# Two preact attention layers in float32: one-pass sums, a different order of VectorE's additions, and the last batch's order

## The chip, the cores and the metric

The kernel runs on one core of one Trainium2 chip. The metric is the device time of the whole kernel in microseconds, from one launch, as the median of several runs. Lower is better. The core's engines are called as in the profile: PE (TensorE, matrix products), DVE (VectorE), ACT (ScalarE), POOL (GpSimd) and SP (SyncE, which here only issues DMAs).

## The reference

The input x has 8 batches of 32 x 32 positions (1024 tokens) and 512 channels, all float32. Two residual layers follow one another. Each normalises its input over groups of 16 channels, runs an attention and adds the result to its input.

```python
# layer 0: 16 heads of 32
x = x + attention_0(group_norm(x))      # softmax(q k^T * 32**-0.5) v, then @ w_proj + b_proj
# layer 1: 4 heads of 128, relative position logits
x = x + attention_1(group_norm(x))      # q = x @ Wq * 128**-0.5
                                        # scores = q k^T + rel_w(q, pos_w) + rel_h(q, pos_h)
                                        # softmax(scores) v, then @ Wo
```

## The kernel before, in words

**Layout.** Activations are kept transposed, channels on the 128 partitions and 1024 tokens along the row, as blocks of 4 x 1024 (eight such blocks in SBUF). Every projection of a 512 x 512 matrix is done by a seven-product scheme (`seven`, called through `project_T`, `project_rows` and the output projections): the operand is split into quarters a11, a12, a21, a22; `forms` makes four sums of them on DVE (lines 339 to 342, 128x1024 each); seven products, each of half the channels, go to PSUM banks x, y, z in the order 0, 5, 1, 4, 6, 2, 3. One such run makes half the output and is called a unit. Bank y is a running sum: after product 5 DVE reads it (`a`, line 379), then product 4 is added on top and DVE reads it again (`b`, line 387), then product 2. So PE may not start product 4 before `a` has been read. Products 0 and 1 use a11 and a12 alone and need none of the forms.

**First attention** (`attention_0`): 64 steps per batch (4 head groups, 2 halves of the queries, 8 key tiles). A step makes the scores of four heads into the four-bank PSUM tile `ps` (line 539), ACT exponentiates them to `e` (line 547, 128x2048, two buffers, tag `e0`), PE multiplies the `e` of the step before with the values (line 558), and DVE adds that `e` to the running `esum` (lines 567 and 569). After 8 steps the sums over keys are a product with ones (line 579), and `normalise` turns them into factors (lines 502 to 524: an ACT copy, two DVE transposes, a reciprocal, a POOL multiplication).

**Second attention** (`attention_1`): 64 steps per batch (4 heads, 2 halves, 8 key tiles). A step is a float32 product of keys and queries (line 654), a float32r product that adds the position logits (line 655), an exponential (line 657, buffers of tag `e1`, three of them), the values product (line 666) and DVE's addition (lines 675 and 677). Every 8 steps a float32 product with ones (line 686) gives the sums, in one of the three PSUM banks of tag `bank`, followed by `normalise`.

**Order.** The main loop runs nine rounds. In round b, `side_by_side` spreads the rest of the work evenly over the steps of batch b's first attention: the output projection of batch b-1's first layer (`after_0`), that of batch b-2's second layer (`after_1`, with its output transposes at line 856 and the DMAs at line 861), the second norm (`norm_1`, scalings at line 294), the projections of `second`, batch b-1's second attention and the projections of batch b+1. The steps of the second attention have no cost in this spreading, so in most rounds all 64 stand between two steps of the first attention. `load` of the next batch is woven into them, one piece every six steps. Round 7 has no next batch and interleaves the first 32 steps of the second attention with the first attention. Round 8 has only the rest. After it stands the last `after_1`, of batch 7. Weights are loaded by SP some products ahead (lines 193 and 197), in program order with SP's other DMAs: outputs, inputs, and the copies of x put away in DRAM (line 218) and fetched back (line 225).

**Queues.** [...] The framework orders instructions from the program and from dependences; `tc.issue_after(x)` keeps what it encloses behind x.

**Start.** `load_first` loads batch 0 in rows, transposes it on PE (line 744), copies it from PSUM (lines 752 and 754), takes statistics (line 249), puts x away, normalises in place (line 294) and makes the forms. `add_up` (line 146) makes the four differences of each weight matrix that the seven products need.

## Time and profile before

| | us |
|---|---|
| median of 3 runs | 3877.97 (3873.93 to 3879.32) |
| the profiled execution | 3877.0 |
| its span, first to last instruction | 3875.2 |
| PE busy | 3803.0 (98%) |
| DVE busy | 2516.4 (65%) |
| ACT busy | 1723.9 (44%) |
| POOL busy | 625.1 (16%) |
| TensorE clock granted, mean | 0.996 |

A row of the page or of an answer names the line of the kernel, the engine, the operation, what it writes and from what, with tile names. `x512` counts instructions; busy time and mean duration follow, then the idle time of the engine just ahead and what ended it. In the timeline the first number is the start, the second the time taken, and a bracket at the end gives idle time before and its releaser. A float32 product appears as two records. Records of PE overlap in time, [...] so a busy PE can still hide short waits.

### The profile page before, as it was taken

What the parts mean: (1) busy time and instruction counts of PE and PEld (TensorE: products, weight loads), DVE (VectorE), ACT (ScalarE), POOL (GpSimd) and SP (SyncE); (2) the same over time, 40 slices, a digit from 0 to 9 for tenths busy, and PEclk for the clock granted to TensorE, in tenths of its full rate; (3) what the DMA queues carried; (4) which work ended last, traced back from release to release, by engine and by line L of the source; (5) the groups of instructions that cost most, each with busy time, mean ns of one, the idle gap of its engine ahead of it and who ended that gap; (6) DMA issues with size and microseconds to landing.
All of it is one profiled execution on the core that took longest, in us unless ns stands there. A gap on an engine that the chain in (4) does not pass through costs nothing.

```text
span 3875.2 us, 79813 instructions
## 1 busy us (share of the span) xinstructions
PE 3803.0 (98%) x34478; PEld 1375.0 (35%) x34478; DVE 2516.4 (65%) x2905; ACT 1723.9 (44%) x1767; POOL 625.1 (16%) x400
## 2 busy tenths in 40 slices
PE   8999999999999999999999999999999999999998
PEld 3222244232443234432343323433234332334353
DVE  6777765686745867468664686656866568665544
ACT  2554543545434454344544445444453445553232
POOL 2242101121001211012111121111210112001101
PEclk9999999999999999999999999999999999999999
DMA  6122120142202322033120241103311023110401
GB/s 183 58 87 80 42 60 3 37 126 65 57 6 79 94 54 55 12 92 87 42 55 17 92 94 38 47 21 98 90 41 39 27 97 76 34 52 24 121 17 23
DMA packets 482984, 234.73 MB, mean 61 GB/s; under 512 B 269600, under 2 KB 461376, under 8 KB 481600
## 3 DMA queue, kind: packets, MB, share of 16 engines
q1 hardware_dynamic: 470992, 213.74, 20.4%
q0 software_dynamic: 2608, 13.70, 1.0%
q8 instruction: 274, 4.49, 0.5%
q10 hardware_dynamic: 9024, 2.10, 0.3%
q14 instruction: 86, 0.70, 0.1%
HBM read 170.72 MB, written 58.72 MB: 59 GB/s over the span
## 4 chain that ended last, share of the span: by engine, by line
PE 87%; DVE 8%; ACT 2%; issue 2%; DMA 0%; SPq 0%; POOL 0%; DVEq 0%; ACTq 0%; POOLq 0%
PE ps L539 12%; PE ps L654 11%; PE acc L666 11%; PE acc L558 11%; PE y_q L315 4%; PE y_v L315 4%; PE y_k L315 4%; PE ps L655 3%; PE x_q L315 3%; PE z_k L315 3%; PE x_v L315 3%; PE x_k L315 3%; PE z_q L315 3%; PE z_v L315 3%; DVE es L569 2%; ACT e L547 2%
## 5 line engine op out<-in xcount | busy, mean ns | idle before, releaser
L547 ACT ACTIVATE e<-ps 128x2048 f32<-128x2048 f32 x512 | 961.6, 1878 | 839.3 <-PE ps L539 628.2
L569 DVE TENSOR_TENSOR es<-es,e 128x2048 f32<-128x2048 f32 x384 | 893.3, 2326 | 408.6 <-ACT e L547 405.6
L539 PE MATMUL ps<-q,k 32*64 32x512 f32 x8192 | 576.6, 614 | 18.4 <-ACT e L547 18.4
L657 ACT ACTIVATE e<-ps 128x512 f32<-128x512 f32 x512 | 305.7, 597 | 573.8 <-PE ps L655 537.8
L558 PE MATMUL acc<-e,v 128*32 128x512 f32 x4096 | 545.9, 605 | 0.0
L654 PE MATMUL ps<-q,k 128*128 128x512 f32 x1024 | 525.2, 595 | 0.3 <-DVE posT L640 0.3
L666 PE MATMUL acc<-e,v 128*128 128x512 f32 x1024 | 522.0, 593 | 0.0
L524 POOL TENSOR_TENSOR q<-q,su 128x512 f32<-128x512 f32 x128 | 216.3, 1690 | 1556.8 <-DVE su L520 1538.0
L677 DVE TENSOR_TENSOR es<-es,e 128x512 f32<-128x512 f32 x384 | 290.6, 757 | 252.8 <-ACT e L657 250.8
L655 PE MATMUL ps<-posT,sel 128*128 128x512 f32 x512 | 407.0, 795 | 0.0
L654 PEld LDWEIGHTS ps<-q,k 128*128 128x128 f32 x1024 | 192.9, 190 | 250.4 <-issue 243.8
L539 PEld LDWEIGHTS ps<-q,k 32*64 32x64 f32 x8192 | 120.3, 130 | 409.8 <-issue 221.1
L666 PEld LDWEIGHTS acc<-e,v 128*128 128x128 f32 x1024 | 193.5, 190 | 146.3 <-issue 105.0
L558 PEld LDWEIGHTS acc<-e,v 128*32 128x32 f32 x4096 | 81.5, 108 | 412.0 <-issue 364.7
L567 DVE TENSOR_TENSOR es<-e,e 128x2048 f32<-128x2048 f32 x64 | 172.9, 2701 | 33.2 <-ACT e L547 33.2
L504 DVE STREAM_TRANSPOSE tu<-su 128x512 f32<-128x512 f32 x128 | 90.6, 708 | 121.7 <-ACT su L502 120.1
L502 ACT COPY su<-sums 128x512 f32<-128x512 f32 x128 | 74.9, 585 | 149.0 <-PE sums L579 81.2
L655 PEld LDWEIGHTS ps<-posT,sel 128*128 128x128 f32 x512 | 97.5, 190 | 122.3 <-issue 122.3
L640 DVE TENSOR_TENSOR posT<-pp,posT 32x512 fp32r<-32x512 f32 x128 | 112.0, 875 | 32.3 <-ACT posT L635 31.0
L675 DVE TENSOR_TENSOR es<-e,e 128x512 f32<-128x512 f32 x64 | 44.2, 691 | 135.8 <-ACT e L657 135.8
L428 POOL TENSOR_TENSOR k<-b_k,p_k 128x512 f32<-128x512 f32 x32 | 51.9, 1623 | 483.6 <-ACT p_k L393 483.6
L635 ACT CAST posT<-pp 32x512 fp32r<-32x512 f32 x128 | 106.2, 829 | 46.3 <-PE pp L622 45.1
(200 smaller groups left out, 4449.4 us busy)
## 6 DMA issues: line engine op xcount, KB each, us to landing
w_qkv<-ws_qkv SPq DMA_DIRECT2D x168, 128.0 KB, 2.5
d<-x0T SPq DMA_DIRECT2D x32, 512.0 KB, 3.6
x1T<-d SPq DMA_DIRECT2D x32, 512.0 KB, 5.4
d<-x1T SPq DMA_DIRECT2D x32, 512.0 KB, 3.4
x2T<-d SPq DMA_DIRECT2D x32, 512.0 KB, 6.0
w_qkv<-in_L_conv_w_qkv SPq DMA_DIRECT2D x126, 128.0 KB, 2.2
out<-ot SPq DMA_DIRECT2D x240, 64.0 KB, 2.0
xs<-in_x SPq DMA_DIRECT2D x224, 64.0 KB, 2.5
```

The costliest lines, as they stand in the source:

```text
L315: ins = nc.tensor.matmul(out[columns, :], weights[:, columns], moving, start=start, stop=stop, skip_group_check=open_sum,)
L524: nc.gpsimd.tensor_tensor(dst, dst, su, op=ALU.mult)
L539: nc.tensor.matmul(ps[some, r, :], k[m][rows, j * P + 64 * i : j * P + 64 * i + 64], q[m][rows, h * NB : (h + 1) * NB], start=True, stop=True,
L547: nc.scalar.activation(e, ps, AF.Exp, scale=D0 ** -0.5)
L558: nc.tensor.matmul(acc[r * D0 : (r + 1) * D0, :], v[:, j, c0 : c0 + D0], e[:, r, :], start=(j == blocks[0]), stop=(j == blocks[-1]),)
L567: nc.vector.tensor_add(state["esum"], state["first"], e)
L569: nc.vector.tensor_add(state["esum"], state["esum"], e)
L654: nc.tensor.matmul(ps, k[h][:, keys], q[:, h, queries], start=True, stop=False)
L655: nc.tensor.matmul(ps, sel_flat[:, keys], posT[:, h, queries], start=False, stop=True)
L657: nc.scalar.activation(e, ps, AF.Exp, scale=1.0 / math.sqrt(D1))
L666: nc.tensor.matmul(acc, v[:, j, h * D1 : (h + 1) * D1], e, start=(j == 0), stop=(j == NT - 1),)
L677: nc.vector.tensor_add(state["esum"], state["esum"], e)
```

## The change

It has seven parts.

1. `finish` in the second attention, for all but the first three sums of round 7: ACT copies `esum` to a float32r tile (`greater`), DVE subtracts that from `esum` into another (`rest`), and two float32r products with ones replace the float32 one. They go to the tile `ps` and are issued two steps later.
2. Additions of the first attention (`esum`) are issued behind the last `a` or `b` (`reader`).
3. The scalings of the second norm are each issued behind the last such addition (`summed`), from round 2 on.
4. The forms of a loaded batch are made one at a time, each behind the last addition of the second attention (`added`); `load` is woven in with gap 5 instead of 6.
5. Batch 6's output (transposes and DMAs) is put off and woven into the last second attention.
6. Batch 7's output projection runs products 0 and 1 of both units ahead of the forms, then the other five of each.
7. At the start, all copies of the transposed rows are on ACT, the statistics take chunks in the order 0, 2, 1, 3, and the weight differences of two matrices come behind the forms.

```diff
+    ones_r = consts.tile([P, P], F32R, tag="ones", name="ones")
+    nc.gpsimd.memset(ones_r.bitcast(F32), 1.0)
+    ones = ones_r.bitcast(F32)
...
+    FIRST_TWO, LAST_FIVE = [0, 1], [5, 4, 6, 2, 3]
...
-    def forms(x, name, room=None):
+    def forming(x, name, room=None, behind=None):
...
+        for op, out, one, other in (
+            (nc.vector.tensor_add, s1, a21, a22),
+            (nc.vector.tensor_sub, s2, s1, a11),
+            (nc.vector.tensor_sub, a21, a11, a21),
+            (nc.vector.tensor_sub, s4, a12, s2),
+        ):
+            late = behind() if behind is not None else None
+            with tc.issue_after(late.ins) if late is not None else nullcontext():
+                last_form[0] = op(out, one, other)
+            yield 0
...
-        begun[0] = nc.vector.tensor_add(a, y, p1)
+        reader[0] = begun[0] = nc.vector.tensor_add(a, y, p1)
...
-        half_done[0] = nc.vector.tensor_add(b, y, p1)
+        reader[0] = half_done[0] = nc.vector.tensor_add(b, y, p1)
...
+    def two_first(fs, u, sink, name):
+        product = taken(fs, u, False)
+        x = bank(f"x_{name}")
+        product(x, 0, True)
+        p1 = snapshot("e1", f"p1_{name}")
+        nc.scalar.copy(p1, x)
+        product(x, 1, False)
+        sink.c11(x)
+        return p1
+
+    def five_last(fs, u, sink, name, p1):
+        product = taken(fs, u, False)
+        y = bank(f"y_{name}")
+        product(y, 5, True)
+        a = snapshot("es1", f"a_{name}")
+        nc.vector.tensor_add(a, y, p1)
+        sink.early(p1, a)
+        product(y, 4, False)
+        b = snapshot("es1", f"b_{name}")
+        nc.vector.tensor_add(b, y, p1)
+        sink.middle(b)
+        z = bank(f"z_{name}")
+        product(z, 6, True)
+        p7 = snapshot("e1", f"p7_{name}")
+        nc.scalar.copy(p7, z)
+        product(y, 2, False)
+        sink.c12(y, p1)
+        product(z, 3, False)
+        sink.c21(z, a)
+        sink.c22(b, p7)
...
-                nc.vector.tensor_add(state["esum"], state["first"], e)
+                other = state["first"]
             elif j != blocks[0]:
-                nc.vector.tensor_add(state["esum"], state["esum"], e)
+                other = state["esum"]
+            if j != blocks[0]:
+                with tc.issue_after(reader[0].ins):
+                    summed[0] = nc.vector.tensor_add(state["esum"], other, e)
...
-            su = bank(f"sums_{name}")
-            nc.tensor.matmul(su, ones, esum, start=True, stop=True)
+            if (h * NH + c + 1) * NT < beside:
+                su = bank(f"sums_{name}")
+                nc.tensor.matmul(su, ones, esum, start=True, stop=True)
+                normalise(q[:, h, c * NB : (c + 1) * NB], su, name)
+                return
+            yield
+            greater = mem.tile([P, NB], F32R, tag="rec", name=f"sg_{name}", bufs=2)
+            nc.scalar.copy(greater, esum)
+            rest = mem.tile([P, NB], F32R, tag="rec", name=f"sr_{name}", bufs=2)
+            nc.vector.tensor_sub(rest, esum, greater.bitcast(F32))
+            yield
+            yield
+            su = psum.tile([P, HB, NB], F32, tag="ps", name=f"sums_{name}", bufs=1)[:, 0, :]
+            nc.tensor.matmul(su, ones_r, greater, start=True, stop=False)
+            nc.tensor.matmul(su, ones_r, rest, start=False, stop=True)
             normalise(q[:, h, c * NB : (c + 1) * NB], su, name)
...
-        st["xn"] = forms(x, f"xn0_{b}")
+        st["xn"] = yield from forming(x, f"xn0_{b}", behind=lambda: added[0])
...
-                if h == 0 or cc % 2:
-                    nc.scalar.copy(part, banks[cc])
-                else:
-                    nc.vector.tensor_copy(part, banks[cc])
+                nc.scalar.copy(part, banks[cc])
...
-        for cc in (1, 0, 3, 2):
+        for cc in (0, 2, 1, 3):
             statistics(st, xT, cc, "0_0")
...
+            late = b == B - 2
+            with tc.issue_after(added[0].ins) if late else nullcontext():
+                nc.vector.transpose(ot, xT[m][:, h * NB : (h + 1) * NB])
...
+    def late_output(st):
+        for put in st.pop("late"):
+            put()
+            yield 0
+
+    def after_last(b, st):
+        x = st["ao"]
+        xT = fetch(st["kept"], block(f"x2T_{b}"))
+        sinks = [Onto(halves(xT, u), then=put_out(b, st, xT, u)) for u in range(2)]
+        early = [x[:, :HC, :NB], x[:, HC:, :NB]]
+        p1s = []
+        for u in range(2):
+            stream.unit(WO, False, u)
+            p1s.append(two_first(early, u, sinks[u], f"wo_{b}_{u}"))
+        fs = forms(x, f"ao1_{b}")
+        for u in range(2):
+            stream.unit(WO, False, u)
+            five_last(fs, u, sinks[u], f"wo_{b}_{u}", p1s[u])
...
-        m.add_up(nc.vector, nc.gpsimd, keep=True)
+        with tc.issue_after(last_form[0].ins):
+            m.add_up(nc.vector, nc.gpsimd, keep=True)
...
-                norm = norm_1(b - 1, last, after=lambda: half_done[0])
+                norm = norm_1(
+                    b - 1, last, after=lambda: half_done[0], behind=lambda: summed[0]
+                )
...
-            rest.append(woven(attention, incoming, 4, 6))
+            if here is None:
+                incoming = later(late_output, past)
+            rest.append(woven(attention, incoming, 4, 5))
...
-    run(after_1(B - 1, states[B - 1]))
+    after_last(B - 1, states[B - 1])
```

## The prediction

> **What bounds the kernel now.** I read the page first, for the engine that carries the span.

> ```profile
> span 3875.2 us, 79813 instructions
> PE 3803.0 (98%) x34478; PEld 1375.0 (35%) x34478; DVE 2516.4 (65%) x2905; ACT 1723.9 (44%) x1767; POOL 625.1 (16%) x400
> PE 87%; DVE 8%; ACT 2%; issue 2%; DMA 0%; SPq 0%; POOL 0%; DVEq 0%; ACTq 0%; POOLq 0%
> ```

> TensorE is busy 98% of the span, and the chain that ended last lies 87% on it. So only two things can shorten the run: less matmul time, or fewer waits of TensorE. The waits of the PE engine list the second kind (us in total, times, longest):

> ```profile
> PE ps L539 <- ACT e L547: 18.4, 16, 2.9
> PE x_v L315 <- issue: 10.6, 1, 10.6
> PE y_wo L315 <- DVE a_wo L379: 10.5, 7, 1.7
> PE y_wo L315 <- DVE f_ao L340: 3.1, 1, 3.1
> PE x_q L315 <- DMA w_q<-in_L_conv_Wq: 2.9, 1, 2.9
> ```

> The 18.4 us are first-attention scores waiting for an exponential, itself held by a late addition; 10.6 us are the start, before the first norm is done; 10.5 us are the output projection waiting for one late read of a half-done sum. These are ceilings for whatever the change does to waits. For matmul time I read the timeline of PE in the last shared attention (start, duration):

> ```profile
> 3513.93 1.02 PE L666 MATMUL acc<-e,v 128*128 128x512 f32 x2
> 3514.78 1.02 PE L686 MATMUL sums<-es,ones 128*128 128x512 f32 x2
> 3515.64 1.02 PE L654 MATMUL ps<-q,k 128*128 128x512 f32 x2
> 3516.10 0.80 PE L655 MATMUL ps<-posT,sel 128*128 128x512 f32 x1
> 3516.73 1.02 PE L666 MATMUL acc<-e,v 128*128 128x512 f32 x2
> ```

> Durations overlap, so starts are subtracted. The float32 sum at L686 costs 3515.64 - 3514.78 = 0.86 us. From L654 to the next L666 are 1.09 us; less another 0.86 for L654, the one-pass float32r matmul at L655 costs 0.23 us. The second attention has no gap there: each step is PE alone.

> Third, the timeline around the 10.5 us:

> ```profile
> 863.21 4.65 DVE L569 TENSOR_TENSOR es<-es,e 128x2048 f32<-128x2048 f32 x2
> 867.77 0.69 DVE L379 TENSOR_TENSOR a_wo<-y_wo,p_wo 128x512 f32<-128x512 f32 x1
> 868.51 1.92 PE L315 MATMUL y_wo<-f_ao,w_o 128*32 128x512 f32 x16 [1.42 <-DVE a_wo L379]
> ```

> Two long additions stand ahead of a short read, and PE stands still 1.42 us; the same occurs near 1341, 1814, 2288 and 2761 us.

> [...] The trace shows half clock after a 2.92 us wait, in the windows view (PEclk 0.51):

> ```profile
> 3629.10:3632.50 3.40, 3.40 (x18) 1.05 (x22) 0.00 (x0) 0.00 (x0) 0.00 (x0) 0.51 0.85 239
> ```

> So that wait cost another 1.7 us. [...] At the end one form takes 2.27 us beside a GpSimd addition and its neighbour 1.23.

> **The change, part by part.**

> 1. *Sums of the second attention.* 61 of 64 L686 products become two float32r products: 0.86 - 2 x 0.23 = 0.40 us less. For the 53 that lie inside an attention this is net, 21.2 us. Their new work is one ACT copy (0.59, row L502) and one DVE subtraction (0.69, as row L677) per 16 us; in that stage DVE is busy 68 of 120 us and ACT 43, and the product comes two steps later, so it is hidden. They use the four-bank `ps` slot, idle there since first attention's steps stand outside. The last sum of each of the first seven attentions has no step behind it: addition, copy, subtraction, product. From the exponential's end these are 0.7 + 0.65 + 0.75 = 2.1 us, beside which PE has 0.86 of values product, then, by the built order, one single 32-column product of the next projection. That product, alone, breaks a group of four. I count 0.64 us lost each (products end at 4.99 instead of 4.35 us), 4.5 us. Bounds: 0 to 10. Net 16.7.
> 2. *Additions behind readers; scalings apart.* In the built VectorE order, L569 moves behind the next `a` or `b`, and the four scalings of L294 (2.98 us at 852.3) fall into two pairs with an addition between. At 866 us one addition of 2.29 us leaves the queue ahead of `a_wo`, and two scalings (1.5 us) enter, but the addition before comes 3 us sooner. I take 8 of the 10.5 us. Of the 18.4 us, 0.98 us at each of five batches follow the scalings: 4.9, and 0.6 elsewhere: 5.5. The rest lies in the first two batches, where the order hardly changes. Bounds: 3 to 25.
> 3. *Batch 6's output moved into the last attention.* 8 transposes (0.70 each, 5.6 us of DVE) and 32 output DMAs (SP needs 5.35 us for nine) leave the stage at 3580 to 3632. The output issues stood ahead of weight loads on SP:

> ```profile
> SPq L861 <- DVE ot L856: 264.6, 36, 146.4
> ```

>  The loads for the x_q at 3629 were issued only at 3626.66, hence 2.9 us plus 1.7 at half clock: 4.6 gained. In the last attention DVE is busy 52 of 124 us, and in the built order SP issues the last weights and x2T ahead of these outputs, so nothing waits for them. A transpose held behind an addition delays only additions, by at most a step (1.94 us), and three `e1` buffers cover it. Bounds: 2 to 6.
> 4. *The start.* Two copies go from DVE to ACT, and eight weight additions (four of them, 3.6 us and a 2.2 us DMA wait, inside the chain of statistics) go behind the forms. The chain would end 6.5 us earlier, near 19.5 instead of 26.36. But scaling is in place and must wait for the writes `d<-x0T`, and a weight load of 1 MB now precedes these on SP: at the 402 GB/s of the window 17 to 27.3 us it adds 2.6. They landed by 14.6 + 7.4 = 22; now about 25.8, so scalings end near 26 instead of 29.3: 3.5 gained. Bounds: 0 to 6.5.
> 5. *The end.* The first two products of both halves need no forms: four of 1.72 us now run while the forms are made.

> ```profile
> 3836.80 2.27 DVE L339 TENSOR_TENSOR f_ao<-q 128x1024 f32<-128x1024 f32 x1 [1.10 <-POOL q L524]
> 3840.39 3.31 PE L315 MATMUL y_wo<-f_ao,w_o 128*32 128x512 f32 x16 [3.14 <-DVE f_ao L340]
> ```

>  y_wo would start near 41.5 instead of 40.4: the sum's chain is longer (0.7) and one GpSimd addition (1.26) now precedes L524. But then ten products remain, 17.2 us and about 1.5 of waits for `a` and `b`: 60.2 against 64.98. 4.5 gained. Bounds: 0 to 8.
> 6. *Slower pace and forms one by one* (gap 5, twelve pieces instead of nine): the last form falls at step 59 of 64, 9.7 us before it is wanted: nothing; if that cover were gone, y_q would wait next. New waits elsewhere, unnamed: 2 us off.

> Sum: 16.7 + 8 + 5.5 + 4.6 + 3.5 + 4.5 - 2 = 40.8, say 41. The profiled execution took 3877.0 us (1.8 beyond its span): 3836. The median shown, 3877.97, is 1.0 higher: **3837**.

> **Rivals.**

> - *Everything late goes.* All 18.4 and 10.5 us vanish, start and end give their upper bounds, the last sums cost nothing: 21 + 29 + 6 + 6.5 + 8 = 70, so about 3808. For it: DVE is busy only 65%, so lateness is order. Against: the start is DMA-bound, and the first batches keep their order.
> - *Only the sums pay.* Part 2 only moves waits (the 2.29 us addition is late for the sum over four heads, L579, instead), last sums lose 10: 21 - 10 + 3 + 2 = 16, so 3862. For it: L579 already waited for L569 twice (3.1 us).
> - *Head-of-line blocking: slower.* An addition behind `a` or `b` waits for a projection product even when its exponential is ready; behind it stand all VectorE reads, behind those the exponential that reuses one of two `e0` buffers, then L539. There are 113 units beside first attention, 226 such readers. At 0.18 us each the gain of 41 is gone; at 0.30, 68 us are lost: 3905. Against: there is slack. The addition for the exponential at 521.24 ended at 525.44, while the buffer's next exponential began at 534.22: 8.8 us. For it: where DVE is full (35 of 40 us near 860 to 900) that slack is used up.
> - *The change doesn't act.* Ruled out for the sums (the built PE order shows the new pairs); for the additions the order moves, but if every read was in time anyway, part 2 is worth 3 and the result 3847, inside the first case.

> **How the numbers follow.** A change under 0.2% (7.8 us) can't be told from none. First case 0.61 (own range 3822 to 3852), everything 0.15, only the sums 0.14 (of it 0.03 within 0.2%), blocking 0.10 (of it 0.01 within 0.2%). Faster 0.61 + 0.15 + 0.11 = 0.87, same 0.04, slower 0.09. The range takes the other faster cases but their ends: 3806 to 3868.

> **What would show it.** In the profile after: L686's row down to 3 products, new pairs costing 0.46 us between starts; `y_wo <- a_wo` under 4 us; no wait of x_q on w_q near 3590; first x_v two to five us earlier; y_wo at the end within 3 us of the fourth x_wo product. The forecast is wrong if PE's wait for `e L547` rises above 18.4 us, or if the attention's step is no longer 1.94 us.

## The result, and the profile after

The changed kernel takes 3902.94 us (median of 4 runs, 3900.45 to 3904.69) against 3876.78 us (3873.93 to 3879.32) of the kernel before: a ratio of 1.0069, 95% interval 1.0056 to 1.0083. It is **slower** by 26 us; the forecast was 41 us faster. The profiled execution has a span of 3902.9 us, 27.7 more than before.

The page of the changed kernel, as read first before:

```profile
span 3902.9 us, 79909 instructions
PE 3804.2 (97%) x34478; PEld 1378.1 (35%) x34478; DVE 2555.9 (65%) x2964; ACT 1760.7 (45%) x1830; POOL 701.6 (18%) x400
PE 85%; DVE 9%; ACT 3%; issue 1%; DMA 1%; SPq 0%; POOL 0%; DVEq 0%; ACTq 0%; POOLq 0%
```

The chain still lies on TensorE, but the parts of DVE and ACT rose by one point each. The waits of the PE engine (us in total, times, longest) say where:

```profile
PE ps L599 <- ACT e L607: 49.5, 37, 4.1
PE sums L643 <- DVE es L633: 18.3, 12, 2.2
PE x_v L323 <- issue: 5.2, 1, 5.2
...
PE y_wo L323 <- DVE a_wo L407: 1.6, 1, 1.6
```

The waits that the change was read to remove did go: y_wo for a_wo fell from 10.5 to 1.6 us (and 1.0 at the reordered end, L449), the first x_v from 10.6 to 5.2, and x_q no longer waits for w_q. But the scores' wait for the exponential rose from 18.4 to 49.5 us, and the first attention's sums now wait 18.3 us (3.1 before) for the last addition. That is the sign by which the prediction said it would be wrong.

The new sums do what they should. In the timeline of PE in the last attention (start, duration), the time from one L718 to the next is 1.95 us without a sum, as before, and 2.42 us with one:

```profile
3816.04 1.02 PE L718 MATMUL ps<-q,k 128*128 128x512 f32 x2
...
3817.99 1.02 PE L718 MATMUL ps<-q,k 128*128 128x512 f32 x2
3818.45 0.80 PE L719 MATMUL ps<-posT,sel 128*128 128x512 f32 x1
3819.08 1.02 PE L730 MATMUL acc<-e,v 128*128 128x512 f32 x2
3819.53 0.80 PE L766 MATMUL sums<-sg,ones 128*128 128x512 f32 x1
3820.17 0.40 PE L767 MATMUL sums<-sr,ones 128*128 128x512 f32 x1
3820.41 1.02 PE L718 MATMUL ps<-q,k 128*128 128x512 f32 x2
```

A step with a sum took 2.81 us before (1.95 and the 0.86 of the float32 sum): 0.39 us less, for 0.40 in the prediction. What the title calls one-pass is in the trace a float32r product of one record (x1), for which the prediction worked out 0.23 us from starts, against two records (x2) and 0.86 us for a float32 one; how many passes either takes is not shown. From the start of its first step to that of its last, an attention that stands alone takes 125.2 us instead of 127.9.

One of the new waits in full, in the timeline around 2241 us:

```profile
2240.81 1.11 PE L599 MATMUL ps<-q,k 32*64 32x512 f32 x16
...
2240.95 0.69 DVE L415 TENSOR_TENSOR b_wp<-y_wp,p_wp 128x512 f32<-128x512 f32 x1 [0.24 <-PE y_wp L323]
2241.56 2.28 DVE L633 TENSOR_TENSOR es<-e,e 128x2048 f32<-128x2048 f32 x1
...
2243.93 1.88 ACT L607 ACTIVATE e<-ps 128x2048 f32<-128x2048 f32 x1 [5.50 <-DVE es L633]
...
2245.86 0.69 PE L599 MATMUL ps<-q,k 32*64 32x512 f32 x8 [1.22 <-ACT e L607]
```

Read it from the bottom. TensorE stands 1.22 us waiting for the exponential. The exponential's scores were done at 2241.92, but it started only at 2243.93: ACT stood idle 5.50 us in all, and what released it was the addition at L633, which gave it a buffer. That addition ran only behind `b_wp`, whose product came at 2240.9; the later of the two exponentials that it adds had ended at 2238.44. It is the **first** addition of a sum, `es <- e,e`: it reads the first two exponentials, and until it is done both `e0` buffers are taken. The same picture stands near 2190, with `b_k` and 3.00 us of VectorE's idle time ahead of it.

VectorE's waits show the size of the blocking:

```profile
DVE es L633 <- ACT e L607: 199.1, 154, 2.6
DVE b_k L415 <- PE y_k L323: 110.3, 32, 5.1
DVE b_v L415 <- PE y_v L323: 109.6, 32, 5.0
```

Idle time ahead of additions fell (the first attention's waited 438.8 us for exponentials before), and idle time ahead of `a` and `b` rose: over all rows of these reads from 265 to 537 us. VectorE has 39 us more work, the new subtractions (42 us). Its idle time has moved to reads whose product is not there yet, and in the two stretches above an addition that could run stood behind such a read. Of these 272 us TensorE feels about a sixth, the 46 us by which its two waits grew.

### The profile page after: what moved, and what is told of

It is laid out like the page before. It is cut to its first block, busy times and chain, and to the rows that moved or that the text cites. A ratio compares the mean times of both kernels' runs of the same rounds, so it can differ in the third digit from the quotient of the medians.

```text
span 3902.9 us, 79909 instructions
## 1 busy us (share of the span) xinstructions
PE 3804.2 (97%) x34478; PEld 1378.1 (35%) x34478; DVE 2555.9 (65%) x2964; ACT 1760.7 (45%) x1830; POOL 701.6 (18%) x400
## 4 chain that ended last, share of the span: by engine, by line
PE 85%; DVE 9%; ACT 3%; issue 1%; DMA 1%; SPq 0%; POOL 0%; DVEq 0%; ACTq 0%; POOLq 0%
PE ps L599 12%; PE ps L718 11%; PE acc L730 11%; PE acc L618 11%; DVE es L633 4%; PE y_k L323 4%; PE y_q L323 4%; PE y_v L323 4%; PE ps L719 3%; PE x_k L323 3%; PE z_q L323 3%; PE x_v L323 3%; PE x_q L323 2%; PE z_k L323 2%; PE z_v L323 2%; ACT e L607 2%
## 5 line engine op out<-in xcount | busy, mean ns | idle before, releaser
L633 DVE TENSOR_TENSOR es<-es,e 128x2048 f32<-128x2048 f32 x384 | 891.5, 2322 | 184.6 <-ACT e L607 179.7
L599 PE MATMUL ps<-q,k 32*64 32x512 f32 x8192 | 582.0, 617 | 49.5 <-ACT e L607 49.5
L718 PE MATMUL ps<-q,k 128*128 128x512 f32 x1024 | 525.1, 594 | 0.5 <-DVE posT L704 0.3
L584 POOL TENSOR_TENSOR q<-q,su 128x512 f32<-128x512 f32 x128 | 197.2, 1540 | 1578.7 <-DVE su L580 1459.8
L718 PEld LDWEIGHTS ps<-q,k 128*128 128x128 f32 x1024 | 192.5, 190 | 230.8 <-issue 219.3
L633 DVE TENSOR_TENSOR es<-e,e 128x2048 f32<-128x2048 f32 x64 | 167.3, 2615 | 19.4 <-ACT e L607 19.4
L488 POOL TENSOR_TENSOR k<-b_k,p_k 128x512 f32<-128x512 f32 x32 | 62.0, 1938 | 490.8 <-ACT p_k L421 490.8
L488 POOL TENSOR_TENSOR v<-b_v,p_v 128x512 f32<-128x512 f32 x32 | 60.8, 1900 | 442.5 <-ACT p_v L421 439.8
```

Of the source, the lines that this page charges most:

```text
L488: nc.gpsimd.tensor_tensor(self.dst[1][1], s(b), s(p7), op=ALU.add)
L584: nc.gpsimd.tensor_tensor(dst, dst, su, op=ALU.mult)
L599: nc.tensor.matmul(ps[some, r, :], k[m][rows, j * P + 64 * i : j * P + 64 * i + 64], q[m][rows, h * NB : (h + 1) * NB], start=True, stop=True,
L633: summed[0] = nc.vector.tensor_add(state["esum"], other, e)
L718: nc.tensor.matmul(ps, k[h][:, keys], q[:, h, queries], start=True, stop=False)
```

## The experiments

The theory (H): the hold, part 2 of the change, blocks VectorE's queue, and the rest of the change works about as forecast. The rival (R): the new sums in `ps`, the scalings apart or the quicker pace of `load` make the waits. Each kernel ran beside the kernel before, whose medians were 3875.95, 3877.48 and 3876.01 us in the three groups of four. Where two of them are compared below, it is by their distance from that.

### One part alone, or taken away

**The changed kernel without the hold**

```diff
-                with tc.issue_after(reader[0].ins):
+                with nullcontext():
                     summed[0] = nc.vector.tensor_add(state["esum"], other, e)
```

> The changed kernel with one part undone: the first attention's additions are no longer issued behind the last read of a half-done sum. Theory H (the hold blocks VectorE's queue, the second exponential behind it waits for its buffer, then the scores): PE's wait for the exponential falls from 49.5 to about 18 us, its wait of the sums for the addition from 18.3 to about 3, the half-clock stretches after the 2.3 us waits go (some 10 us), and the wait of y_wo for a_wo comes back by about 8: 3903 - 31 - 15 - 10 + 8 = 3855 us (3845 to 3868). Rival R (the float32r sums in the tile ps, the scalings apart or the quicker pace of load make the waits): the wait stays above 40 us and the time at 3895 or more.

Measured: 3846.88 us (3846.81 to 3847.79), ratio 0.9926 (0.9912 to 0.9940): 29.1 us faster than before, and 55 us from the changed kernel. Its waits of the PE engine:

```profile
PE ps L599 <- ACT e L607: 14.4, 11, 2.9
PE y_wo L323 <- DVE a_wo L407: 8.6, 6, 1.6
PE x_v L323 <- issue: 5.6, 1, 5.6
```

The scores' wait is below that of the kernel before, the sums' wait for the last addition has left the list, and y_wo's is back. H stands, R falls. The sum of the differences: 35.1 + 18.3 - 7.0 = 46.4 us, and the record of the granted clock has nine stretches of 3.4 us at half clock after the start with the hold and two without it: seven more, at most 1.7 us lost in each, 12 us. Together that is 58 us, and the two spans differ by 57.9. The close fit is partly luck: by span less busy time, TensorE's whole idle time fell by 43.3 us, as some small waits grew.

**The kernel before with the hold alone** (the same `reader` and `issue_after` lines put into it)

> The kernel before with one part added: the hold of the first attention's additions behind the last a or b, nothing else. Theory H: the 46 us of waits and about 10 us of half clock come, 8 us of y_wo's wait go: 3877 + 46 + 10 - 8 = 3925 us (3910 to 3935). Rival R: the hold only moves waits, 3865 to 3882 us.

Measured: 3938.98 us (3933.68 to 3939.58), ratio 1.0162 (1.0149 to 1.0176). The direction is H's, the 63 us more than the 48 expected.

```profile
PE ps L540 <- ACT e L548: 52.8, 37, 4.1
PE sums L583 <- DVE es L573: 18.5, 12, 2.2
```

The two waits are those of the changed kernel. So they need neither the new sums nor the new pace. The profiled execution is the quickest of the five (3933.68 us). In it TensorE's idle time is 38.9 us above that of the kernel before (111.1 against 72.2), and thirteen stretches of 3.4 us at half clock after the start, against four, cost at most another 15 us: 54 of the 57 us between the spans. So the forecast was short mainly in the half clock. The other four executions, 4 to 6 us slower, had a mean granted clock of 0.990 or 0.991, against 0.992 here.

**The kernel before with the new sums alone** (`finish` of the diff, and nothing else)

> The kernel before with one part added: the float32r sums of the second attention in the tile ps. Theory H: 61 products at about 0.39 us less and some 4 us lost at the last sums: 3877 - 17 to 20 = 3858 us (3855 to 3866). Rival R, with the sums guilty (ps taken by a sum makes the next first-attention scores wait): 3877 or more.

Measured: 3874.54 us, ratio 0.9995 (0.9987 to 1.0003). **Neither theory had this**: the sums gain next to nothing alone. Not because `ps` is taken:

```profile
PE ps L540 <- ACT e L548: 18.5, 16, 2.9
PE y_wo L316 <- DVE a_wo L380: 10.5, 7, 1.7
PE x_v L316 <- issue: 10.4, 1, 10.4
PE acc L667 <- ACT e L658: 7.3, 6, 1.3
```

The first line is unchanged. The last is new: in six attentions the values product waits once, 1.2 or 1.3 us, for an exponential of the second attention. The run with the forms in one piece, below, shows why.

**The hold behind `a` alone**

```diff
-        reader[0] = half_done[0] = nc.vector.tensor_add(b, y, p1)
+        half_done[0] = nc.vector.tensor_add(b, y, p1)
```

> The changed kernel with the hold behind a alone, not behind b. Under H each hold costs by the time that VectorE stands waiting for the product; the idle time ahead of all b rows rose by about 126 us and ahead of all a rows by about 142 us between the two profiles, so half of the loss goes: about 3878 us (3868 to 3890), with y_wo's wait for a_wo still under 3 us. Under R it stays at 3895 or more. If only the holds behind b delay exponentials, it comes to 3855 or less.

Measured: 3855.01 us, ratio 0.9946 (0.9933 to 0.9960), 47 us from the changed kernel: below H's range, and at the mark set for the case that only the holds behind `b` delay exponentials. Nearly so: they carry 47 of the 55 us. The idle time of VectorE is no measure of the loss: its growth is split about evenly between `a` (140 us) and `b` (132), and ahead of `a` it is still 243 us here (87 before, 226 with the full hold), though the loss is nearly gone. The wait of the scores is 24.3 us here, 10 above the kernel without any hold, y_wo's is 1.6, and the sum is still 8 us worse than no hold.

### Which hold does the harm

**The hold only behind `a_wo`**, the read that y_wo was waiting for

```diff
-        reader[0] = begun[0] = nc.vector.tensor_add(a, y, p1)
+        begun[0] = nc.vector.tensor_add(a, y, p1)
+        if reader[0] is None or name.startswith("wo"):
+            reader[0] = begun[0]
...
-        reader[0] = half_done[0] = nc.vector.tensor_add(b, y, p1)
+        half_done[0] = nc.vector.tensor_add(b, y, p1)
```

> The changed kernel with the hold kept only behind the output projection's read a_wo of the second layer, the one read that TensorE waited for in the kernel before. Theory H (a hold costs where VectorE then waits for a product, and pays only where a late read is waited for): as without any hold, 3847 us, less most of the 8.6 us that y_wo still waits for a_wo there: about 3840 (3838 to 3845). Rival: every hold makes an exponential late, so what y_wo gains the scores lose: 3846 to 3852.

Measured: 3854.60 us, ratio 0.9944 (0.9930 to 0.9957): the rival's side, and 6 us worse than without any hold.

```profile
PE ps L601 <- ACT e L609: 23.8, 21, 2.9
...
PE y_wo L323 <- DVE b_wo L417: 3.2, 5, 0.6
```

What y_wo gains at `a_wo` (8.6 to 1.6) it half loses at `b_wo` (3.2), and the scores lose 9.4 us. The windows view suggests why: in the kernel without the hold (stretch, its length, then busy time of PE, PEld, DVE, ACT and POOL)

```profile
840.00:860.00 20.00, 20.00 (x216) 4.91 (x208) 19.41 (x27) 8.70 (x6) 9.05 (x6) 1.00 0.38 71
860.00:880.00 20.00, 18.62 (x192) 4.61 (x184) 19.83 (x22) 9.10 (x8) 6.66 (x3) 1.00 0.48 89
```

VectorE is busy 39.2 of 40 us. Whatever is let through first, something else comes late: with this hold, with the one behind `a` above and with the one below that frees first and last additions, y_wo waits 1.6 us for `a_wo` and the scores 21 to 24 us, against 8.6 and 14.4 without a hold.

**All additions held but the first of each sum**

```diff
-                with tc.issue_after(reader[0].ins):
+                with nullcontext() if j == blocks[1] else tc.issue_after(reader[0].ins):
```

> The changed kernel with the hold on all additions but the first of each sum. In the changed kernel's trace 31 of TensorE's 34 waits over 0.3 us for an exponential that came right after an addition lie behind a first addition (es from e and e), which alone frees both e0 buffers. Theory F: so only those holds make exponentials late: the wait falls from 49.5 to 15 to 20 us, the 18.3 us of the sums behind the last addition stay, and y_wo's wait for a_wo stays small: 3903 - 32 - 5 of half clock = 3866 us (3858 to 3875). Rival G: any held addition makes an exponential late; one addition of eight freed gives an eighth of 56 us: 3896 (3890 to 3900).

Measured: 3876.39 us, ratio 1.0002 (0.9993 to 1.0010). F's range ended at 3875 and G's began at 3890, so F is much nearer, but its size was too large: one addition in seven carries 26 of the 55 us.

```profile
PE ps L599 <- ACT e L607: 24.4, 17, 2.9
PE sums L643 <- DVE es L633: 16.4, 11, 2.2
```

The scores' wait fell by 25 us, not by 32, and the sums' wait stayed, as F said. A free first addition can still come late in the full window: in this trace TensorE waits behind one near 882 us and at four more batches, 1.7 to 1.8 us each, as VectorE had other work ahead of it.

**The last addition free too**

```diff
-                with tc.issue_after(reader[0].ins):
+                with nullcontext() if j in (blocks[1], blocks[-1]) else tc.issue_after(reader[0].ins):
```

> As the run before, and the last addition of each sum is free too. Theory F: the wait of the sums for the last addition goes as well, and most of y_wo's 8.6 us stays saved: 3842 us (3838 to 3850), at or under the 3847 of the kernel without any hold. Rival G: two additions of eight freed: 3889 (3880 to 3895). Third possibility: the last addition waits for the one before it, which is still held; then the 18.3 us stay and it is as the run before, some 3866.

Measured: 3855.31 us, ratio 0.9948 (0.9934 to 0.9961): another 21 us.

```profile
PE ps L599 <- ACT e L607: 21.2, 17, 2.9
...
PE sums L643 <- DVE es L633: 3.5, 5, 0.7
```

The sums' wait falls from 16.4 to 3.5 us. First and last additions together carry 47 of the 55 us; the five between them, held as before, cost 8 net of what y_wo gains. The hope of beating the kernel without any hold is not met: what y_wo gains (8.6 to 1.6 us) the scores lose again (14.4 to 21.2). This split of the loss by position in the sum and the split by `a` and `b` above are two cuts through the same 55 us. The last addition was freed only after the first, never alone.

### The other steps, each taken out of the kernel without the hold

**Forms in one piece, `load` every six steps**

```diff
-        st["xn"] = yield from forming(x, f"xn0_{b}", behind=lambda: added[0])
+        st["xn"] = forms(x, f"xn0_{b}")
+        yield 0
...
-            rest.append(woven(attention, incoming, 4, 5))
+            rest.append(woven(attention, incoming, 4, 5 if here is None else 6))
```

> The changed kernel without the hold, and with the loaded batch's forms made in one piece and load woven in every six steps, as before. The prediction counted this part at 0: 3847 us (3844 to 3849). Rival, from the run of the sums alone: with the quicker sums the four forms in a row make six exponentials of the second attention late, PE's wait of the values product for e is 7.3 us again: 3854 us (3851 to 3857).

Measured: 3857.47 us, ratio 0.9951 (0.9938 to 0.9965), 9 us worse.

```profile
PE acc L730 <- ACT e L721: 7.3, 6, 1.3
```

The rival's number is right, and the wait is that of the sums alone, to the tenth. Its reason, that the sums are quicker, is not what the trace shows:

```profile
1058.53 0.79 PE L719 MATMUL ps<-posT,sel 128*128 128x512 f32 x1
...
1060.54 0.68 DVE L741 TENSOR_TENSOR es<-es,e 128x512 f32<-128x512 f32 x1
1061.31 0.62 ACT L758 CAST sg<-es 128x512 fp32r<-128x512 f32 x1 [3.30 <-DVE es L741]
1061.84 0.59 ACT L721 ACTIVATE e<-ps 128x512 f32<-128x512 f32 x1
...
1062.48 1.13 PE L730 MATMUL acc<-e,v 128*128 128x512 f32 x2 [1.21 <-ACT e L721]
```

The scores of the exponential at 1061.84 were done at 1059.32. Ahead of it in ACT's queue stands the copy `sg`, the first piece of the new sum, and the copy waits 3.30 us for the sum's last addition, which VectorE makes late, between forms. All six waits here, and all six in the run of the sums alone, have this order: the copy, idle 3.3 to 3.4 us, and the exponential right behind it. So it is the blocking of the hold once more, on ACT and not meant. The kernel before makes the forms in one piece too, but has no such copy. The forms and the pace were put back together; no run moved the copy.

**Scalings in one piece** (`behind=lambda: summed[0]` left out of the call of `norm_1`)

> The changed kernel without the hold, and with the second norm's four scalings in one piece. The prediction's step 2: the waits of 0.98 us of the scores for e at five batches come back, 4.9 us: 3852 us (3850 to 3855). Rival: without the hold the additions come early anyway and the scalings fall into their place: 3847 us.

Measured: 3854.09 us, ratio 0.9942 (0.9929 to 0.9956), 5.7 us worse; the scores' wait goes from 14.4 to 18.7 us and the time from one attention to the next from 470.2 to 471.2 us. As the prediction's step 2 had it: five waits of 0.98 or 0.99 us are back, one in each of five batches.

**The end as before**

```diff
-    plan += [(WO, False, u, some) for some in (FIRST_TWO, LAST_FIVE) for u in range(2)]
+    plan += units(WO)
...
-    after_last(B - 1, states[B - 1])
+    forms_1(B - 1, states[B - 1])
+    run(after_1(B - 1, states[B - 1]))
```

> The changed kernel without the hold, and with the last batch's output projection in the old order (forms first, then unit by unit). By the prediction 4.5 us are lost; by the traces from the last values product to TensorE's end it took 34.02 us before, 36.13 with the new sums alone and 31.55 with the new end: 4.6 us, so 3851.5 us (3849 to 3854). Rival: the new order gains nothing, since the forms are waited for all the same: 3847 us.

Measured: 3852.19 us, ratio 0.9938 (0.9925 to 0.9952), 3.8 us worse, and y_wo waits 3.7 us for f_ao. From the last step's scores to TensorE's end it takes 37.7 us, with the new order 34.0.

**The old sums** (one float32 product at every eighth step, where the kernel before has it)

> The changed kernel without the hold, and with the second attention's sums as before (one float32 product). The prediction's step 1: the new sums are worth 16.7 us net, so 3864 us (3860 to 3868). Rival, from the run of the sums alone (1.4 us gained): they are worth 1 to 3 us, 3849. Third: with the forms one by one, which take away the 7.3 us of waits that the sums alone brought, 10 to 20: 3857 to 3867.

Measured: 3858.50 us, ratio 0.9957 (0.9943 to 0.9970): the sums are worth 11.6 us here, inside the range of the third expectation.

**Batch 6's output where it was**

```diff
-            late = b == B - 2
+            late = False
...
-        return put_later if b == B - 2 else put
+        return put
...
-            if here is None:
-                incoming = later(late_output, past)
```

> The changed kernel without the hold, and with batch 6's transposes and output DMAs where they were, in the stage before the last attention. The prediction's step 3: x_q waits for its weights again, 2.9 us and 1.7 at half clock: 3851.5 us (3849 to 3854). Rival: the loads would have come in time in this order of the other parts, 3847 us.

Measured: 3853.48 us, ratio 0.9946 (0.9932 to 0.9960), 6.5 us worse.

```profile
PE y_wo L323 <- DVE a_wo L407: 10.3, 7, 1.7
...
PE x_q L323 <- DMA w_q<-in_L_conv_Wq: 2.9, 1, 2.9
```

The x_q wait is back as forecast, but in this execution no half clock followed it (the last section shows the two cases side by side). In its place y_wo waits a seventh time, 1.7 us: three of the transposes stand ahead of an `a_wo` again, between 3584 and 3589 us.

## Why the prediction was wrong

| step | forecast gain, us | measured, us | from |
|---|---|---|---|
| 1 sums | 16.7 | 11.6 (1.4 without step 6) | old sums put back; sums alone |
| 2 additions behind readers | 8 | **-55** | hold taken out |
| 2 scalings apart | 5.5 | 5.7 | scalings in one piece |
| 3 batch 6's output | 4.6 | 6.5 | output where it was |
| 4 start | 3.5 | 2.1 | traces alone |
| 5 end | 4.5 | 3.8 | end as before |
| 6 forms one by one | 0 | 9 (needed by step 1) | forms in one piece |

**The step that failed is the hold in step 2.** Its working followed one addition at one place, 866 us, and counted what leaves the queue ahead of `a_wo`. It did not count what a hold does at all the other readers, which the prediction priced only in its third rival. That rival had the mechanism in its true order (reader, addition, exponential that reuses one of two buffers, scores) and its 3905 us are close to the 3903 measured, but it was given a chance of 0.10. The argument against it was the slack of 8.8 us at one addition near 521 us. That was an addition in the middle of a sum. The first addition frees two buffers at once and has none to spare, the last is awaited by the product with ones. One instance was taken for all 448 additions. The bounds of 3 to 25 us for step 2 had no loss in them, though the profile before spoke for one. Behind 9 of the 15 waits of the scores over 0.25 us there, 12.3 of the 18.4 us, the exponential began within 0.1 us of the end of a first addition (L567), and only 64 of the 448 additions are first ones. The longest of them:

```profile
144.17 2.28 DVE L567 TENSOR_TENSOR es<-e,e 128x2048 f32<-128x2048 f32 x1
146.54 1.88 ACT L547 ACTIVATE e<-ps 128x2048 f32<-128x2048 f32 x1 [5.48 <-DVE es L567]
148.47 1.12 PE L539 MATMUL ps<-q,k 32*64 32x512 f32 x16 [2.92 <-ACT e L547]
```

The rival's even price of 0.30 us for each of 226 readers came near by accident: the 55 us measured are 0.24 for each, and most of the loss sits at two of seven additions and behind `b`.

**Step 6** was read against the wrong consumer. The prediction asked when the last form is wanted; what counts is what the forms hold up while they are made: the sum's last addition, the new copy that waits for it on ACT, and the exponential behind the copy. Step 1 called this copy hidden, since ACT is busy only 43 of 120 us; its place in the queue was left out. The 9 us are not an extra gain: without them the sums gain only 1.4.

**Step 1**: the 0.39 us are right, the losses around them were undersized. Between two attentions the new sums save 1.9 us (472.1 against 470.2), of 2.7 inside one: 0.8 lost, for 0.64. The single product that the prediction saw ahead of the last sum is in the changed kernel's trace: two records of x_q at 675.26 us, and the next product starts 0.98 us later, where sixteen records of x_q take 1.72 us from start to start (685.30 to 687.02). In addition the stretch from the start of the attention in round 7 to that of the last takes 293.5 us with them and 292.0 without, where a gain of about 2 was counted for its five sums, and the tail after the last step is 1.3 us longer. One reason for round 7 stands in the trace of the kernel without the hold. The three float32 sums kept there are issued one step earlier than before, and two of them (at 3406.9 and 3432.2 us) fall into the middle of first-attention scores: two of the sixteen records, the sum, and later the other fourteen. The two take 1.0 us, as long as all sixteen together (1.04), from which each place is estimated at about 1 us. No run separated this.

**Step 4**: the first x_v starts at 21.8 us instead of 27.3 in the kernel without the hold, but a wait that both kernels have, of 0.62 us for an exponential, ends at 112.45 instead of 114.55 us. So 2.1 us are left of 5.5. The mechanism was right and the size was off: the four scalings wait 5.6 us together for the writes `d<-x0T`, and the last ends at 28.0 us, not near 26 (29.3 before). The prediction's own terms, 22 and 2.6 for the weight load ahead of the writes, give 24.6, not the 25.8 that it used; the last scaling could start only at 27.2. An x_v then waits 0.9 us for the scaled `x0T` and a y_v 1.1 us for `f_xn`. No run separated this step.

**Steps 3 and 5** and the scalings hold within 2 us, step 3 with another content: its 1.7 us of half clock did not come back with the wait, 1.7 us of y_wo did. Without the hold the prediction's sum is 40.8 - 8 = 32.8 us; 29.1 were measured, in part because a smaller gain of the sums and a larger one of step 3 offset each other.

The version to keep is the changed kernel without the hold, at 0.9926 of the kernel before; it beats both, and none of the partial holds beats it.

## What to carry to other kernels

In these runs an instruction queued behind another's wait cost little or a lot, depending on who waits for it (the five additions in the middle of a sum 8 us net, the first 26, the last 21): before ordering a whole class of instructions behind something, look for the members with no slack, here the first (which frees two buffers) and the last (which a product awaits), and price those. Whether a third buffer would give the first addition slack was not run. Where an engine is full over a stretch, as VectorE is here (busy 39.2 of 40 us), a new order only moved the wait. An added instruction can block a queue without being meant to, as the copy did on ACT (idle 3.3 to 3.4 us, six times): for each one, ask what stands behind it and how late its input can be. So parts of a change should be priced together where they share an engine.

## What the runs showed of the hardware

The half-clock stretches are not a matter of the wait's length alone. The wait of x_q for its weights is 2.92 us both in the kernel before and in the run with batch 6's output where it was; the sixteen products behind it take 3.62 us in the one and 1.92 in the other. The windows view (PEclk, the granted clock, is the number behind the five engines) of the kernel before:

```profile
3625.74:3629.15 3.41, 0.49 (x9) 0.09 (x8) 0.69 (x1) 0.00 (x0) 0.00 (x0) 1.00 0.70 137
3629.15:3632.57 3.42, 3.42 (x20) 1.07 (x24) 0.00 (x0) 0.00 (x0) 0.00 (x0) 0.50 0.85 239
```

and of that run:

```profile
3606.24:3609.65 3.41, 2.08 (x20) 0.39 (x12) 1.38 (x2) 0.00 (x0) 0.70 (x1) 1.00 0.82 121
3609.65:3613.07 3.42, 1.83 (x20) 0.77 (x24) 0.00 (x0) 0.00 (x0) 0.00 (x0) 1.00 0.72 196
```

It also sorts the five rounds of the changed kernel in which TensorE stands still 2.2 us for the last addition of a first-attention sum. In three of them the wait lies in one cell but for at most 0.1 us (TensorE busy 36 to 40% of it, 1.2 to 1.4 of 3.41 us), and the next cell is at half clock. In two it is split over a border (busy 56% of the emptier cell), and the clock stays at 1.00.

So what the prediction charged for the wait of x_q, 1.7 us at half clock, was read rightly from one trace, but in these traces it goes with the place of the wait on the raster and not with the wait.
